# Cross-attention with layer norm: inverse roots as exp(-ln/2), and a new order for the last six row tiles

## The chip, the core and the metric

The kernel runs on one core of one Trainium2 chip. The metric is the device time of one execution in microseconds (us), lower is better. The engines have instruction queues of their own and meet through semaphores: TensorE (PE in the profile; PEld is its weight load), VectorE (DVE), ScalarE (ACT), GpSimd (POOL), and SyncE (SP), whose queue issues nearly all DMAs.

## The reference

Cross-attention of x (16 batches, 256 rows, 256 columns) to a context of 77 keys of 192 columns, 8 heads of 256, then a residual and a layer norm, all in float32:

```python
Q = (img_embed @ Wq).reshape(B, -1, H, D).transpose(0, 2, 1, 3)
K = (sent_embed @ Wk).reshape(B, -1, H, D).transpose(0, 2, 1, 3)
V = (sent_embed @ Wv).reshape(B, -1, H, D).transpose(0, 2, 1, 3)
score = jnp.einsum('bhqd,bhkd->bhqk', Q, K) / math.sqrt(D)
score = jnp.where(mask, score, -jnp.inf)
attn = jax.nn.softmax(score, axis=-1)
ctx = jnp.einsum('bhqk,bhkd->bqhd', attn, V).reshape(B, -1, H * D)
out = ctx @ Wo + img_embed
mu = jnp.mean(out, axis=-1, keepdims=True)
var = jnp.var(out, axis=-1, keepdims=True)
return (out - mu) * jax.lax.rsqrt(var + EPS) * gamma + beta
```

## The kernel before

**Tiling.** The 4,096 rows of x are 32 tiles of 128 rows, numbered 0 to 31, two to a batch and eight to a group; a group is one buffer `xg`, in which x, the residual sum and the output replace each other in place. The weights are folded first (Wq with Wk into `gA`, `gB`; Wv with Wo into `uA`, `uB`), which takes the first 55 us of the profile.

**The loop.** Lines 854 to 925 run over b from -1 to 14, software-pipelined by batch: `new` are the two tiles of batch b+1, which get scores, softmax and a transpose; `now` are the two of batch b, which get their attention product; `old` are the two of batch b-1, which get their layer norm. In the last iteration, b = 14, `old` is tiles 26 and 27, `now` 28 and 29, `new` 30 and 31. After the loop lines 929 to 945 attend tiles 30 and 31 and normalise 28 to 31. The order in which the program is written is the order on each engine's queue; nothing is rescheduled.

**The steps for one tile t**, with the engine that does each:

- `scores(t)`: 128 matmuls on PE into two PSUM banks.
- `shift(t)`: DVE adds the mask bias (L326, twice) and takes the negated maximum of each head (L333).
- `exponential(t)`: eight Exp on ACT, one for each head (L340).
- `weigh(t)`: DVE sums (L346) and inverts (L348), POOL multiplies (L354, twice).
- `turn(t)`: DVE transposes the weights for the product (L364).
- `attend(t)`: 40 matmuls on PE into one PSUM bank (L376). Batches 0 to 10 use `seven` in its place, a product with fewer multiplications.
- `finish(t)`: DVE adds the product to the residual (`add_product`, L474) where that has not been done, then takes mean and variance (bn_stats L482, bn_aggr L485) into `mv`.
- `spread(first, last)`: ACT takes std = Sqrt(var + eps) of tiles first to last-1 (L493).
- `invert(first, last, aside)`: DVE takes rstd = 1/std (L500); for the tiles in `aside`, `less` = -mean * rstd on POOL, or on the engine given as `less_on` (L504).
- `normalise(t)`: in one of two ways. On DVE alone: `centre` (L514, subtract the mean and multiply by gamma) and L530 (multiply by rstd, add beta), both scalar_tensor_tensor. Or `aside`: ACT applies rstd and `less` (Identity, L524), POOL multiplies by gamma (L525) and adds beta (L526). When both tiles of a batch are done, SP issues their output DMA (L537); the two last tiles have a DMA each (L945).

**ScalarE's tables.** Exp and Sqrt come from different sets of tables. Before an activation whose function is not in the loaded set stands an ACT_TABLE_LOAD; Copy and Identity follow either without one. The one-element Exp into `warm` (L598, L890, L911) brings Exp's set back at a time of the program's choosing.

**The end, in the order of the code.** Iteration 14 on DVE: `shift` 30 and 31, then statistics of 26 between the softmax sums of 30 and 31, those of 27, `turn(30)`, the reciprocal for 26 and 27, `turn(31)`, `finish` 28 and 29. On ACT: 16 Exp, Sqrt for 26 and 27, two copies of the product V*Wo of batch 15 out of PSUM (`vw`, L884), Identity of 26 and 27, Sqrt for 28 and 29. Behind the loop: 28 and 31 are normalised by DVE, 29 and 30 by ACT and POOL.

Of the kernel before, what the change touches and what calls it, by code (L numbers as in the profile page):

```python
# [8 lines left out]
F32 = mybir.dt.float32  # L9
I32 = mybir.dt.int32  # L10
AF = mybir.ActivationFunctionType
# [4 lines left out]
P = 128  # L16
# [37 lines left out]
def kernel(  # L54
# [13 lines left out]
    nc = tc.nc  # L68
    B, S, DI = x.shape
# [3 lines left out]
    NG = B // GB  # L73
    QT = S // P
    NT = B * QT
    GT = GB * QT
# [17 lines left out]
    const = ctx.enter_context(tc.tile_pool(name="const", bufs=1))  # L94
    sp = ctx.enter_context(tc.tile_pool(name="sp", bufs=2))
    st = ctx.enter_context(tc.tile_pool(name="st", bufs=4))
# [4 lines left out]
    eps = const.tile([P, 1], F32, tag="eps", name="eps")  # L101
# [22 lines left out]
    bias = const.tile([P, B, S2], F32, tag="bias", name="bias")  # L124
# [3 lines left out]
    xg_of = {}  # L128

    x_rows = x.rearrange("b (t p) d -> p (b t) d", p=P)  # L130
    out_rows = out.rearrange("b (t p) d -> p (b t) d", p=P)
    c_rows = c.rearrange("b k l -> (b k) l").rearrange("(r p) l -> p r l", p=CR)

    def flat(ap):
        return ap.rearrange("p a b -> p (a b)")
# [19 lines left out]
    xT_of, a_of, vw_of, p_of, mv_of = {}, {}, {}, {}, {}  # L155
# [142 lines left out]
    def turn_last(n):  # L298

        blocks = flat(vr[:, 2 * n : 2 * n + 2])  # L300
        nc.vector.transpose(blocks, blocks)


    def scores(t):
        g = t // GT
        j, bl = t % GT, (t // QT) % GB
        ps = [ps_mm.tile([P, 512], F32, tag="mm", name=f"ps_{t}_{a}") for a in range(2)]
        for m in range(NM):
            for dc in range(2):
                for i in range(NM):  # L310
                    nc.tensor.matmul(  # L311
                        ps[m // 2][i * BK : (i + 1) * BK, m % 2 * 2 * S2 : (m % 2 + 1) * 2 * S2],
                        xT_of[g][:, j * NM + m, dc],
                        flat(a_of[g][:, dc, bl, 2 * i : 2 * i + 2, :]),
                        start=(dc == 0),
                        stop=(dc == 1),
                    )
        ps_of[t] = ps
# [153 lines left out]
    def add_product(t):  # L472
        y = xg_of[t // GT][:, t % GT, :]
        nc.vector.tensor_tensor(y, po_of.pop(t), y, ALU.add)  # L474

    def finish(t):
        if t in po_of:
            add_product(t)
        g, j = t // GT, t % GT
        y = xg_of[g][:, j, :]  # L480
        bn = st.tile([P, 6], F32, tag="bn", name=f"bn_{t}")
        nc.vector.bn_stats(bn, y)  # L482
        if j == 0:
            mv_of[g] = st.tile([P, GT, 2], F32, tag="mv", name=f"mv_{g}", bufs=2)
        nc.vector.bn_aggr(mv_of[g][:, j, :], bn)  # L485

    std_of, rstd_of, done = {}, {}, []

    def spread(first, last):

        g, lo, hi = first // GT, first % GT, (last - 1) % GT + 1
        std = st.tile([P, GT], F32, tag="std", name=f"std_{first}")
        nc.scalar.activation(std[:, lo:hi], mv_of[g][:, lo:hi, 1], AF.Sqrt, bias=eps)  # L493
        std_of[first, last] = std

    def invert(first, last, aside=(), less_on=nc.gpsimd):

        g, lo, hi = first // GT, first % GT, (last - 1) % GT + 1
        rstd = st.tile([P, GT], F32, tag="rstd", name=f"rstd_{first}")
        nc.vector.reciprocal(rstd[:, lo:hi], std_of.pop((first, last))[:, lo:hi])  # L500
        if aside:
            less = st.tile([P, GT], F32, tag="less", name=f"less_{first}")
            for j in (t % GT for t in aside):
                less_on.tensor_scalar(  # L504
                    less[:, j : j + 1], mv_of[g][:, j, 0:1], rstd[:, j : j + 1], -1.0,
                    ALU.mult, ALU.mult,
                )
        for t in range(first, last):
            j = slice(t % GT, t % GT + 1)
            rstd_of[t] = rstd[:, j], less[:, j] if aside else None  # L510

    def centre(t):
        y = xg_of[t // GT][:, t % GT, :]
        nc.vector.scalar_tensor_tensor(  # L514
            y, y, mv_of[t // GT][:, t % GT, 0:1], gam, ALU.subtract, ALU.mult
        )

    def normalise(t, aside=False, centred=False):

        g, j = t // GT, t % GT  # L520
        rstd, less = rstd_of.pop(t)
        y = xg_of[g][:, j, :]
        if aside:
            nc.scalar.activation(y, y, AF.Identity, bias=less, scale=rstd)  # L524
            nc.gpsimd.tensor_tensor(y, y, gam, ALU.mult)  # L525
            nc.gpsimd.tensor_tensor(y, y, bet, ALU.add)  # L526
        else:
            if not centred:
                centre(t)
            nc.vector.scalar_tensor_tensor(y, y, rstd, bet, ALU.mult, ALU.add)  # L530
        if t >= NT - QT:
            return
        done.append(t)
        if t ^ 1 in done:
            t |= 1
            j |= 1
            nc.sync.dma_start(  # L537
                out_rows[:, t + 1 - QT : t + 1, :], xg_of[g][:, j + 1 - QT : j + 1, :]
            )
# [4 lines left out]
    with tc.tile_pool(name="wonce", bufs=1) as wp:  # L544
        first = -(-GB * S2 // CR)
# [48 lines left out]
            load_blocks(wk_blk[:, e], wk_blocks[2 * e + 1])  # L594
            load_blocks(wq_blk[:, e], wq_blocks[2 * e + 1])

        warm = const.tile([P, 1], F32, tag="warm", name="warm")
        nc.scalar.activation(warm, eps, AF.Exp)  # L598

        wvT = wp.tile([P, NF, NL, P], F32, tag="wvT", name="wvT")  # L600
        wo_of = [
# [251 lines left out]
    last = NT - 1  # L853
    for b in range(-1, B - 1):
        old = range(max(b - 1, 0) * QT, b * QT)
        now = range(max(b, 0) * QT, (b + 1) * QT)
        new = range((b + 1) * QT, (b + 2) * QT)
        for t in new:
            scores(t)
        for t in new:  # L860
            shift(t)
        for n in range(0, 2) if b < 0 else range(b + 2, min(b + 3, B // 2)):
            turn_last(n)
        g, n = (b + 1) // GB + 1, (b + 1) % GB
        work = [prepare_vw(b + 1)]
        if g < NG:
            work.append(prepare_a(g, (n,)))
            if n == 0:
                load_xT(g)
                load_x(g)  # L870
        for part_A, _, _ in work:
            part_A()
        for _, part_B, _ in work:
            part_B()
        for i, t in enumerate(new):
            exponential(t)
            if old:
                finish(old[i])
            weigh(t)
        if old:  # L880
            spread(old[0], old[-1] + 1)
        for _, _, copies in work:
            for dst, src in copies():
                nc.scalar.copy(dst, src)  # L884
        if b + 1 < NS:
            differences(b + 1)
        if b < NS:
            if now:
                seven(b)
            nc.scalar.activation(warm, eps, AF.Exp)  # L890
            if old:
                invert(old[0], old[-1] + 1)
                normalise(old[0])
            for t in new:
                turn(t)
            if n >= NF - 2:
                for j in range((n - NF + 2) * GT // 2, (n - NF + 3) * GT // 2, 2):
                    transpose_x(g, j)
            if old:
                normalise(old[1])  # L900
            if now:
                add_seven(b)
            if b + 1 < NS:
                sums(b + 1)
            continue
        for t in now:
            attend(t)
        if b < B - 2:
            invert(old[0], old[-1] + 1, aside=old[:1])
            normalise(old[0], aside=True)  # L910
            nc.scalar.activation(warm, eps, AF.Exp)  # L911
            turn(new[0])
            normalise(old[1])
            turn(new[1])
            for t in now:
                add_product(t)
        else:
            turn(new[0])
            invert(old[0], old[-1] + 1, aside=old)
            for t in old:  # L920
                normalise(t, aside=True)
            turn(new[1])
            for t in now:
                finish(t)
            spread(now[0], now[-1] + 1)

    for t in new:
        attend(t)  # L930
    centre(last - 3)
    invert(last - 3, last - 1, aside=(last - 2,), less_on=nc.vector)
    normalise(last - 2, aside=True)
    finish(last - 1)
    spread(last - 1, last)
    normalise(last - 3, centred=True)
    invert(last - 1, last, aside=(last - 1,), less_on=nc.vector)
    normalise(last - 1, aside=True)
    finish(last)
    spread(last, NT)  # L940
    centre(last)
    invert(last, NT)
    normalise(last, centred=True)
    for t, queue in ((last - 1, nc.scalar), (last, nc.sync)):
        queue.dma_start(out_rows[:, t, :], xg_of[NG - 1][:, t % GT, :])  # L945


# [29 lines left out]
```

## Time and profile before

| | |
|---|---|
| time, median of 4 runs | 277.99 us (277.84 to 278.28) |
| the profiled execution | 278.28 us, of which the span is 276.5 us |
| PE busy | 267.3 us, 97% of the span |
| DVE busy | 208.6 us, 75% |
| ACT busy | 165.4 us, 60% |
| POOL busy | 159.6 us, 58% |
| table loads on ACT | 28 of 1,283 ns: 14 for L493, 10 for L890, 3 for L911, 1 for L598 |

Time outside the span (1.78 us here) is what lies around the profiled instructions. A line of the timeline gives start and length in us, then engine, line, operation, output and inputs with their shapes; what stands in brackets at its end is how long the engine had been idle and who released it. Instructions of one engine that don't depend on each other overlap by some tens of nanoseconds, so a start can lie ahead of the end before it.

### The profile page before, as it was taken

Reading aid. Unit: us, or ns where it says so; the run is one execution under the profiler, and the core shown is the slowest. Engines: PE = TensorE matmul, PEld = TensorE weight load, DVE = VectorE, ACT = ScalarE, POOL = GpSimd, SP = SyncE. Lnnn points to the kernel's source line nnn. Section 1 sums busy time; section 2 is a strip of 40 time slices with the busy share of each in tenths; the row PEclk is TensorE's granted clock in tenths of the full one; section 3 lists DMA queues with packets and bytes.
Section 4 is the critical chain, followed back from the end, with each engine's and each line's share of the span. In section 5 each row is a group of like instructions: output and inputs, shape, how many; then the busy total and the mean of one; then the engine's idle time right before and its main releaser. Section 6 shows DMA issues by size and latency. Waiting matters only on the chain.

```text
span 276.5 us, 13238 instructions
## 1 busy us (share of the span) xinstructions
PE 267.3 (97%) x5908; PEld 190.6 (69%) x5908; DVE 208.6 (75%) x423; ACT 165.4 (60%) x443; POOL 159.6 (58%) x221
## 2 busy tenths in 40 slices
PE   6899999999999999999999999999999999999991
PEld 6756587876494949595958586868676767575660
DVE  0453866787748989878789887777788887788885
ACT  2303122255729585867676776768685857869762
POOL 1000004948677777787867878777777536235184
PEclk9999999999999999999999999999999999999998
DMA  6995988892000101930100009500001010110103
GB/s 178 238 206 166 323 125 175 240 200 103 4 6 2 43 2 46 226 119 4 43 2 16 29 5 196 187 6 30 17 2 40 5 40 6 39 41 2 40 4 114
DMA packets 40201, 22.61 MB, mean 82 GB/s; under 512 B 23168, under 2 KB 38608, under 8 KB 40144
## 3 DMA queue, kind: packets, MB, share of 16 engines
q1 hardware_dynamic: 40000, 21.64, 31.9%
q8 instruction: 46, 0.75, 1.1%
q10 hardware_dynamic: 144, 0.13, 0.1%
q14 instruction: 11, 0.09, 0.1%
HBM read 17.57 MB, written 4.19 MB: 79 GB/s over the span
## 4 chain that ended last, share of the span: by engine, by line
PE 87%; DVE 4%; DMA 3%; ACT 2%; POOL 1%; SPq 1%; issue 1%; POOLq 0%; ACTq 0%
PE ps L311 24%; PE pa L197 12%; PE pv L239 9%; PE po L427 9%; PE pm L427 7%; PE pa L211 6%; PE pv L250 6%; PE po L376 5%; DMA c_sb<-in_ctx_dram 3%; PE pu L701 3%; ACT e L340 2%; PE pw L715 1%; PE pgb L701 1%; PE pr L282 1%; PE pr L272 1%; POOL uB L827 1%
## 5 line engine op out<-in xcount | busy, mean ns | idle before, releaser
L340 ACT ACTIVATE e<-s,top 128x77 f32<-128x77 f32 x256 | 67.2, 347 | 51.8 <-DVE top L333 49.6
L354 POOL TENSOR_TENSOR p<-e,rden 128x512 f32<-128x512 f32 x64 | 45.8, 738 | 46.0 <-DVE rden L348 40.6
L311 PE MATMUL ps<-a,xT 128*32 128x154 f32 x2048 | 70.0, 294 | 0.0
L311 PEld LDWEIGHTS ps<-a,xT 128*32 128x32 f32 x2048 | 66.1, 110 | 1.7 <-issue 0.8
L326 DVE TENSOR_TENSOR s<-ps,bias 128x308 f32<-128x308 f32 x64 | 30.4, 474 | 16.9 <-PE ps L311 16.8
L197 PE MATMUL pa<-cA,gA 128*32 128x308 f32 x512 | 35.8, 423 | 0.0
L460 POOL TENSOR_TENSOR xg<-xg,m 128x256 f32<-128x256 f32 x33 | 24.2, 733 | 13.5 <-DVE xg L474 11.8
L197 PEld LDWEIGHTS pa<-cA,gA 128*32 128x32 f32 x512 | 16.4, 110 | 20.9 <-issue 7.9
L239 PE MATMUL pv<-uA,cA 128*32 128x512 f32 x256 | 30.4, 592 | 0.0
L364 DVE STREAM_TRANSPOSE pT<-p 128x640 f32<-128x640 f32 x32 | 25.6, 825 | 2.6 <-POOL p L354 2.6
L346 DVE TENSOR_REDUCE den<-e 128x8 f32<-128x616 f32 x32 | 24.7, 772 | 3.2 <-ACT e L340 3.2
L333 DVE TENSOR_REDUCE top<-s 128x8 f32<-128x616 f32 x32 | 25.4, 795 | 1.1
L390 POOL TENSOR_TENSOR ts<-vw 128x768 f32<-128x768 f32 x11 | 22.0, 1998 | 0.0
L211 PE MATMUL pa<-cB,gB 64*32 64x308 f32 x512 | 19.5, 420 | 0.0
L376 PE MATMUL po<-vw,pT 128*32 128x256 f32 x320 | 19.2, 380 | 0.0
L884 ACT COPY vw<-pv 128x512 f32<-128x512 f32 x32 | 16.9, 578 | 2.7 <-PE pv L250 2.7
L493 ACT ACT_TABLE_LOAD x14 | 18.0, 1283 | 0.3
L211 PEld LDWEIGHTS pa<-cB,gB 64*32 64x32 f32 x512 | 9.7, 107 | 11.3 <-issue 7.6
L250 PE MATMUL pv<-uB,cB 64*32 64x512 f32 x256 | 17.4, 601 | 0.0
L514 DVE SCALAR_TENSOR_TENSOR xg<-xg,mv,gam 128x256 f32<-128x256 f32 x25 | 17.2, 688 | 0.0
L884 ACT COPY a<-pa 128x308 f32<-128x308 f32 x48 | 16.6, 446 | 0.0
L376 PEld LDWEIGHTS po<-vw,pT 128*32 128x32 f32 x320 | 10.0, 110 | 9.5 <-DVE den L346 2.5
(118 smaller groups left out, 415.5 us busy)
## 6 DMA issues: line engine op xcount, KB each, us to landing
xT<-in_x_dram SPq DMA_DIRECT2D x16, 256.0 KB, 7.1
xg<-in_x_dram SPq DMA_DIRECT2D x4, 1024.0 KB, 7.7
out_dram<-xg SPq DMA_DIRECT2D x15, 256.0 KB, 2.1
wo<-in_L_xattn_Wo_dram SPq DMA_DIRECT2D x4, 512.0 KB, 6.3
wvT<-in_L_xattn_Wv_dram SPq DMA_DIRECT2D x16, 96.0 KB, 3.4
wq_nat<-in_L_xattn_Wq_dram SPq DMA_DIRECT2D x2, 512.0 KB, 6.4
wq_blk<-in_L_xattn_Wq_dram SPq DMA_DIRECT2D x8, 128.0 KB, 5.3
wk_blk<-in_L_xattn_Wk_dram SPq DMA_DIRECT2D x8, 96.0 KB, 5.8
```

Of the source, the lines that this page charges most:

```text
L197: nc.tensor.matmul(flat(o[i * BK : (i + 1) * BK]), gA[:, h, cols(dc, i)], flat(cA[:, batches, :]), start=not B_first, stop=B_first,)
L211: nc.tensor.matmul(flat(banks[j + k][i * BK : (i + 1) * BK]), gB[half(k), h % NF, cols(dc, i)], flat(cB[half(k), batches, :]), start=B_fir ...
L239: nc.tensor.matmul(pv[k][i * BK : (i + 1) * BK], cA[:, b, k * BK : (k + 1) * BK], uA[:, parts, :, i], start=True, stop=False,)
L250: nc.tensor.matmul(pv[k][i * BK : (i + 1) * BK], cB[half(k), b, k * BK : (k + 1) * BK], uB[half(k), parts, :, i], start=False, stop=True,)
L311: nc.tensor.matmul(ps[m // 2][i * BK : (i + 1) * BK, m % 2 * 2 * S2 : (m % 2 + 1) * 2 * S2], xT_of[g][:, j * NM + m, dc], flat(a_of[g][:, ...
L326: nc.vector.tensor_tensor(s[:, a * H // 2 : (a + 1) * H // 2], ps[a][:, : H // 2 * S2].rearrange("p (h k) -> p h k", k=S2), bias[:, b, :]. ...
L340: nc.scalar.activation(e[:, h], s[:, h], AF.Exp, bias=top[:, h : h + 1])
L354: nc.gpsimd.tensor_tensor(part, e_mh[:, :, :, keys], rden_mh.unsqueeze(3).to_broadcast(list(part.shape)), ALU.mult,)
L364: nc.vector.transpose(pT_of[t].rearrange("p n m q -> p m n q"), p.rearrange("p m (n k) -> p m n k", k=BK),)
L376: nc.tensor.matmul(po[i * BK : (i + 1) * BK], pT[:, n, i], vw_of[b][:, 2 - n // 2 * 2 : 4 - n // 2 * 2, n % 2, :] if n < NF else vr[:, b, ...
L427: nc.tensor.matmul(out[i * BK : (i + 1) * BK], weight[:, i], moving, start=(n == 0), stop=(n == len(terms) - 1),)
L884: nc.scalar.copy(dst, src)
```

## The change

- `spread` takes, in place of one Sqrt, a Ln of var + eps and an Exp of -0.5 times that, which is rstd itself. The reciprocal in `invert` goes; `invert` only makes `less`.
- The table set `natural_log_exp_and_others` is asked for once, at the start; the three warm Exp are gone.
- In iteration 14, `finish`, `spread`, `invert` and `normalise` of tiles 26 and 27 (both aside, `less` on POOL) stand between the scores and `shift` of tiles 30 and 31.
- The rest of iteration 14: `turn(30)`, `finish(28)`, `spread` of 28 alone, `turn(31)`.
- Behind the loop, 28 and 29 are normalised aside (ACT and POOL, `less` on DVE), one after the other, each with a spread of its own; 30 and 31 are each finished, spread, centred and normalised on DVE, and both output DMAs are issued by SP, each behind its tile.

```diff
     def spread(first, last):
         g, lo, hi = first // GT, first % GT, (last - 1) % GT + 1
-        std = st.tile([P, GT], F32, tag="std", name=f"std_{first}")
-        nc.scalar.activation(std[:, lo:hi], mv_of[g][:, lo:hi, 1], AF.Sqrt, bias=eps)
-        std_of[first, last] = std
+        log = st.tile([P, GT], F32, tag="log", name=f"log_{first}")
+        rstd = st.tile([P, GT], F32, tag="rstd", name=f"rstd_{first}")
+        nc.scalar.activation(log[:, lo:hi], mv_of[g][:, lo:hi, 1], AF.Ln, bias=eps)
+        nc.scalar.activation(rstd[:, lo:hi], log[:, lo:hi], AF.Exp, scale=-0.5)
+        all_rstd_of[first, last] = rstd
     def invert(first, last, aside=(), less_on=nc.gpsimd):
-        g, lo, hi = first // GT, first % GT, (last - 1) % GT + 1
-        rstd = st.tile([P, GT], F32, tag="rstd", name=f"rstd_{first}")
-        nc.vector.reciprocal(rstd[:, lo:hi], std_of.pop((first, last))[:, lo:hi])
+        g = first // GT
+        rstd = all_rstd_of.pop((first, last))
...
-        warm = const.tile([P, 1], F32, tag="warm", name="warm")
-        nc.scalar.activation(warm, eps, AF.Exp)
+        nc.scalar.preload_act_table_set("natural_log_exp_and_others")
...
         for t in new:
             scores(t)
+        if b == B - 2:
+            for t in old:
+                finish(t)
+            spread(old[0], old[-1] + 1)
+            invert(old[0], old[-1] + 1, aside=old)
+            for t in old:
+                normalise(t, aside=True)
         for t in new:
             shift(t)
...
         for i, t in enumerate(new):
             exponential(t)
-            if old:
+            if old and b < B - 2:
                 finish(old[i])
             weigh(t)
-        if old:
+        if old and b < B - 2:
             spread(old[0], old[-1] + 1)
...
-            nc.scalar.activation(warm, eps, AF.Exp)
...
-            nc.scalar.activation(warm, eps, AF.Exp)
...
         else:
             turn(new[0])
-            invert(old[0], old[-1] + 1, aside=old)
-            for t in old:
-                normalise(t, aside=True)
+            finish(now[0])
+            spread(now[0], now[1])
             turn(new[1])
-            for t in now:
-                finish(t)
-            spread(now[0], now[-1] + 1)
     for t in new:
         attend(t)
-    centre(last - 3)
-    invert(last - 3, last - 1, aside=(last - 2,), less_on=nc.vector)
-    normalise(last - 2, aside=True)
-    finish(last - 1)
-    spread(last - 1, last)
-    normalise(last - 3, centred=True)
-    invert(last - 1, last, aside=(last - 1,), less_on=nc.vector)
-    normalise(last - 1, aside=True)
-    finish(last)
-    spread(last, NT)
-    centre(last)
-    invert(last, NT)
-    normalise(last, centred=True)
-    for t, queue in ((last - 1, nc.scalar), (last, nc.sync)):
-        queue.dma_start(out_rows[:, t, :], xg_of[NG - 1][:, t % GT, :])
+    add_product(last - 2)
+    for t in (last - 3, last - 2):
+        invert(t, t + 1, aside=(t,), less_on=nc.vector)
+        normalise(t, aside=True)
+        if t < last - 2:
+            finish(t + 1)
+            spread(t + 1, t + 2)
+    for t in (last - 1, last):
+        finish(t)
+        spread(t, t + 1)
+        centre(t)
+        invert(t, t + 1)
+        normalise(t, centred=True)
+        nc.sync.dma_start(out_rows[:, t, :], xg_of[NG - 1][:, t % GT, :])
```

More of the change, by code (lines that the diff above doesn't have):

```diff
@@ L485, in finish @@
         nc.vector.bn_aggr(mv_of[g][:, j, :], bn)
-    std_of, rstd_of, done = {}, {}, []
+    all_rstd_of, rstd_of, done = {}, {}, []
     def spread(first, last):
         g, lo, hi = first // GT, first % GT, (last - 1) % GT + 1
-        std = st.tile([P, GT], F32, tag="std", name=f"std_{first}")
-        nc.scalar.activation(std[:, lo:hi], mv_of[g][:, lo:hi, 1], AF.Sqrt, bias=eps)
-        std_of[first, last] = std
+        log = st.tile([P, GT], F32, tag="log", name=f"log_{first}")
[3 more added lines that the diff above has]
+        all_rstd_of[first, last] = rstd
     def invert(first, last, aside=(), less_on=nc.gpsimd):
-        g, lo, hi = first // GT, first % GT, (last - 1) % GT + 1
-        rstd = st.tile([P, GT], F32, tag="rstd", name=f"rstd_{first}")
-        nc.vector.reciprocal(rstd[:, lo:hi], std_of.pop((first, last))[:, lo:hi])
+        g = first // GT
+        rstd = all_rstd_of.pop((first, last))
         if aside:
```

## The prediction

> **What bounds the kernel now.** First the busy times and the costliest groups:
>
> ```profile
> PE 267.3 (97%) x5908; PEld 190.6 (69%) x5908; DVE 208.6 (75%) x423; ACT 165.4 (60%) x443; POOL 159.6 (58%) x221
> L493 ACT ACT_TABLE_LOAD x14 | 18.0, 1283 | 0.3
> ```
>
> PE is the bound by far, and ACT, from which the change takes table loads, has 40% to spare. Whether the last stage differs is told by the chain of work that ended last (start, length, work):
>
> ```profile
> 247.82 1.72 PE pv L239 x16
> 249.54 1.02 PE pv L250 x16
> 250.56 4.45 PE po L376 x80
> 255.01 2.14 PE ps L311 x64
> ...
> 258.57 2.05 ACT e L340 x8
> ...
> 265.39 0.84 DVE pT L364
> 266.23 0.32 DVE xg L474
> ...
> 271.22 0.34 DVE xg L474
> ...
> 273.04 0.75 DVE xg L530
> ```
>
> From 49.4 to 257.15 this chain is matmuls without a gap. What other engines do up to there is hidden, as long as PE gets its operands. Then it passes through the softmax of 30 and 31 to `turn(31)` at 265.39, and from there to 273.79 it is DVE alone. So 8.4 us of the span are DVE's, and what leads to `turn(31)` decides their start. The timeline of the end gives the prices:
>
> ```profile
> 254.34 0.48 DVE L530 SCALAR_TENSOR_TENSOR xg<-xg,rstd,bet 128x256 f32<-128x256 f32 x1
> 262.79 1.28 ACT L493 ACT_TABLE_LOAD   x1
> 264.08 0.30 ACT L493 ACTIVATE std<-mv,eps 128x2 f32<-128x2 f32 x1
> 270.09 0.61 PE L376 MATMUL po<-vr,pT 128*32 128x256 f32 x8
> 271.93 0.72 POOL L525 TENSOR_TENSOR xg<-xg,gam 128x256 f32<-128x256 f32 x1 [0.45 <-ACT xg L524]
> 272.26 0.67 DVE L514 SCALAR_TENSOR_TENSOR xg<-xg,mv,gam 128x256 f32<-128x256 f32 x1
> 272.73 0.78 POOL L526 TENSOR_TENSOR xg<-xg,bet 128x256 f32<-128x256 f32 x1
> 273.04 0.75 DVE L530 SCALAR_TENSOR_TENSOR xg<-xg,rstd,bet 128x256 f32<-128x256 f32 x1
> 273.82 0.35 SPq L945 DMA_DIRECT2D out_dram<-xg  x1
> ```
>
> PE ends at 270.70, so nothing after the change can add tile 31's product before about 270.76. DVE's L514 and L530 take 0.44 and 0.48 alone (minima 0.442 and 0.484 of 25), but 0.67 and 0.75 here. Both end 0.28 after the POOL instruction that they overlap (272.65 and 273.51), and so do L514 at 268.12 and L530 at 270.09: the DVE instruction gets going when POOL's has ended. From L530's end to the span's end it is 2.71.
>
> **The change, part by part.** *Table loads.* 28 loads become one: 27 x 1.283 = 34.6 us of ACT time, and 15 warm Exp of 0.20. Cover: the PE chain up to 257.15. The loads of the last stage (255.09 and 262.79) stand in idle time of ACT or behind the last exponential, with the `vw` copies done at 265.34 and wanted at 266.20. Price on the path: 0. Were ACT the bound, it would be the 34.6.
>
> The Trainium skill (*ScalarE: Activation LUTs*, section "What ACT_TABLE_LOAD costs") charges a drain of 1,380 ns for each switch besides the 1,283. The Sqrt above starts 0.01 behind its load, so the row shows no drain; by the page the switches would be worth 72 us of ACT in place of 34.6, and on the path 0 by either.
>
> *Ln and Exp for Sqrt and reciprocal.* Neither is in the trace. Ln has the operands of the Sqrt, 0.295; bounds 0.20 (one-column Exp of L890) and 0.60 (Identity on 256 columns). The Exp has the form of L890's, 0.20; upper bound 0.35 (L340). It reads what Ln wrote, and dependent neighbours elsewhere start 0.03 after the end. From the start of bn_aggr: 0.21 to Ln, 0.295, 0.03, 0.20, 0.05 to the consumer: 0.79. DVE no longer waits 0.57 for std (L500, 13 times); in the loop that is hidden by PE.
>
> *Tiles 26 and 27 ahead of the exponentials.* Iteration 13 first: `turn(28)` need not wait for rstd, so it starts at 252.37 in place of 253.12. `centre(25)` and L530 then meet POOL's products of 29, which costs about 0.35 of that. I take 0.35 as left (bounds 0 and 0.4): `finish(26)` starts at F = 256.15 - 0.35 = 255.8, where `shift(30)` stood. Two finishes are 2 x 0.56 = 1.12 of DVE, and `shift(30)` is queued behind them; its second half waits for PE to 257.17 anyway, so the maxima of 30 end near 258.7 (before: 258.49). On ACT, 16 exponentials are now queued behind the normalise: bn_aggr of 27 starts at F+1.02, Ln +0.21, Exp +0.32, `less` on POOL +0.28, Identity +0.30 (265.33 to 265.63), and +1.0 for two of them: F+3.13 = 258.93. Call s the delay of the first exponential: 258.93 - 258.57 = 0.36, taken as 0.4. The maxima alone would give 0.15, F at 256.15 gives 0.7. POOL's four instructions for 26 and 27 run from 258.6 to 261.7, in its idle 5.49 before the product of 30. Their DMA goes out near 261.7 in place of 269.45, on an idle SP: 0. DVE loses the statistics that stood ahead of the sums of 30, so these start at 261.04 either way.
>
> *Up to tile 31's product.* `turn(31)` comes at 265.39+s by POOL's product, or by DVE's own queue (`turn(30)`, add, bn_stats, bn_aggr of 28: 263.75 + s + 0.72 + 0.42 + 0.46 + 0.10) at T = 265.45+s. PE wants its output at 268.36: slack 2.9 less its 0.84, so PE doesn't wait. The `vw` copies move ahead, as 1.58 of load and Sqrt go. From T: turn 0.77, add of 29 0.33, `less` of 28 at L = T+1.10. POOL then multiplies and adds for 28 from L+0.93 and for 29 from L+2.43 (0.25 to Identity, 0.68 to POOL, pitch 0.81 and 0.69). DVE: `less` of 29 waits for its Exp until L+1.37, add of 30 L+1.50 (or 268.6, when PE has it), statistics, `centre(30)` at L+2.61. That is behind POOL's product of 29, which lasts to L+3.16: `centre` ends at L+3.43. L530 of 30 starts at L+3.46, behind POOL's add of 29, which ends near L+4.01: done at L+4.29. The add of 31 follows at A = L+4.21 = 270.75+s = 271.15. Before: 271.13. So one pair of DVE instructions still meets POOL, and two reciprocals, a `less` and the statistics ahead of the sums are paid for by s.
>
> The Trainium skill speaks against this order: *SBUF — State Buffer*, section "Who interferes with whom", has a VectorE instruction with two SBUF inputs fully blocked for the whole of a GpSimd instruction that started first. The four endings above agree; in the worst phase by the page each of the two would lose all of POOL's 0.73, or 1.46 together, where I have 0.38+0.35.
>
> *The tail.* Before, from the add of 31: 0.45+0.46 to bn_aggr, 1.00 to L530, 0.75: 2.66. After, POOL is done at L+4.01 = 270.96, so `centre(31)` and L530 run alone: 0.45+0.46, 0.79 to 0.86 to rstd (Sqrt came 0.28 behind the last bn_aggr), 0.485: 2.2. L530 ends at 271.15+2.2 = 273.35 in place of 273.79: -0.44.
>
> *Output.* SP issues 28/29 near 271.0 and 30 near 271.4 (0.37 each), so both are clear of 31's issue. Before, the 128 KB of 30 and 31, issued 0.27 apart, shared the DMA engines from 274.4 to 275.2. Alone, the last should land about 0.1 earlier (bounds 0 and 0.3). -0.10.
>
> Sum: -0.44 - 0.10 = -0.54, or s - 0.94 in general: break-even at s = 0.94. The profiled execution would take 278.28 - 0.54 = 277.74; it lies 0.29 above the median, so the forecast for the median is **277.45**.
>
> **The rivals.** *A, more is gained.* `centre(30)` comes 0.2 earlier and goes ahead of POOL's product of 29; then its L530 ends at L+3.85, and A falls to PE's bound of 270.76: -0.93, 277.06. For it: the two are 0.18 apart in my sum. Against: the add of 30 can't start before 268.6.
>
> *B, the gain is eaten.* F stays at 256.15 and the normalise of 26 and 27 holds ACT a little longer: s = 0.9, 277.95. For it: the 0.35 of iteration 13 is my softest number.
>
> *C, slower.* The place is ACT's queue ahead of the first exponential of 30. Costs: F late (0.40), `less` at 0.48, as four of the five on POOL took about that, with the second Identity behind it (0.21), Ln and Exp at their high bounds, some 0.7 with pitch. From 0.31 that makes s = 1.62, +0.68: 278.67. It decides from s = 0.94 and shows as slower from s = 1.5. Against: all three have to come together.
>
> *D, it doesn't do what it says.* If Ln and Exp were still served from two sets, each of the five last spreads would pay 2 x 1.283. One stands ahead of the exponentials (s = 3.0), one behind the last bn_aggr: 3.0 - 0.94 + 2.57 = +4.6, 282.6 at least. For it: nothing in the trace shows such a set. Against: Copy and Identity already follow either Exp or Sqrt without a load.
>
> **How the numbers follow.** Forecast 0.52, its own range 277.1 to 277.8; A 0.18, B 0.14, C 0.13, D 0.03. A measurement of this kernel tells about 0.2%, 0.56 us, from no change. The forecast lies on that edge: 0.30 of its 0.52 below 277.43, 0.22 above. Faster: 0.30+0.18 = 0.48; same: 0.22+0.14 = 0.36; slower: 0.16. The range reaches from A with a shorter Ln (276.95) to between B and C (278.35).
>
> **What would show it.** One ACT_TABLE_LOAD in all; the first exponential of 30 near 258.97; `turn(31)` near 265.85 with PE unbroken to 270.70; L514 and L530 of 31 at 0.44 and 0.48, of 30 at 0.7 or more; L530 of 31 ending near 273.35. I am wrong if PE pauses ahead of 270.70, if POOL still works on 29 after 272, or if s is over 0.94.

## The result, and the profile after

The changed kernel is slightly slower: 278.9 us (median), against 278.2 us for the kernel before on the same chips. The ratio is 1.0025, with a 95% interval of 1.0014 to 1.0035. The profiled execution took 278.63 us with a span of 276.8 us (before: 278.28 and 276.5), so the span shows +0.3, about half of the +0.7 in the medians. The forecast was a ratio of 277.45/277.99 = 0.9981: the wrong direction, and 278.9 lies outside the range.

The page of the changed kernel begins as the change says. ACT is busy for 131.9 us in place of 165.4, and the group of table loads that stood at L493 is gone. The third line is new to the story: "q1" is the DMA queue that carries all data, and its last column is the time that its packets took, as a share of 16 engines' span. "q8" is taken here for the queue that brings PE its instructions, in blocks: 46 packets of 16 KB, about 257 of PE's 5,908 matmuls and 5,908 weight loads to each.

```profile
PE 267.9 (97%) x5908; PEld 191.4 (69%) x5908; DVE 210.2 (76%) x406; ACT 131.9 (48%) x419; POOL 160.3 (58%) x221
...
q1 hardware_dynamic: 40144, 21.77, 35.7%
q8 instruction: 46, 0.75, 1.2%
```

The same line of the page before:

```profile
q1 hardware_dynamic: 40000, 21.64, 31.9%
```

Nearly the same bytes took 35.7% in place of 31.9%. The change adds no transfer: the 144 packets are those of tile 30's output, which ScalarE's queue issued before and SP issues now. Something made the packets themselves slower.

**The end got shorter, as forecast.** The timeline of the changed kernel, for the instructions that the prediction put times to:

```profile
259.94 4.10 ACT L340 ACTIVATE e<-s,top 128x77 f32<-128x77 f32 x16
...
266.71 0.81 DVE L364 STREAM_TRANSPOSE pT<-p 128x640 f32<-128x640 f32 x1
...
270.25 0.73 POOL L526 TENSOR_TENSOR xg<-xg,gam 128x256 f32<-128x256 f32 x1
270.79 0.48 DVE L515 SCALAR_TENSOR_TENSOR xg<-xg,mv,gam 128x256 f32<-128x256 f32 x1
271.06 0.80 POOL L527 TENSOR_TENSOR xg<-xg,bet 128x256 f32<-128x256 f32 x1
271.37 0.77 DVE L531 SCALAR_TENSOR_TENSOR xg<-xg,rstd,bet 128x256 f32<-128x256 f32 x1
...
273.19 0.48 DVE L515 SCALAR_TENSOR_TENSOR xg<-xg,mv,gam 128x256 f32<-128x256 f32 x1
273.19 0.29 ACT L494 ACTIVATE log<-mv,eps 128x1 f32<-128x1 f32 x1 [1.87 <-DVE mv L485]
273.51 0.20 ACT L495 ACTIVATE rstd<-log 128x1 f32<-128x1 f32 x1
273.77 0.48 DVE L531 SCALAR_TENSOR_TENSOR xg<-xg,rstd,bet 128x256 f32<-128x256 f32 x1
```

DVE's L515 and L531 of tile 31 take 0.48 each (0.67 and 0.75 before), side by side with Ln and Exp on ACT. From the end of PE's last matmul to the end of the span it is 276.8 - 271.73 = 5.07, where it was 276.5 - 270.70 = 5.80: **0.73 less**.

**But PE comes to the end 1.03 later** (271.73 against 270.70). The chain of waits says where. The changed kernel, in the iteration that starts its `seven` product (L427) near 118 us:

```profile
118.06 1.88 PE pm L427 x64
119.94 1.40 PE po L427 x49
121.34 0.53 issue
121.87 0.97 PE po L427 x28
```

The kernel before, same place:

```profile
118.11 1.88 PE pm L427 x64
119.99 2.18 PE po L427 x80
122.18 4.19 PE ps L311 x128
```

Before, the 80 matmuls follow each other in 2.18. After, PE stops in the middle of a group, behind the 49th of 80, waiting for nothing that the profile shows: no semaphore wait is seen. PE restarts slowly too (28 matmuls in 0.97, 35 ns each, against 27 ns before), and what follows in this iteration comes 1.09 later against the start of `pm` than before. PE had begun its first scores 0.05 earlier, and nothing later makes the rest good: +1.03 - 0.73 = +0.3, the difference of the spans.

At that time the DMA engines are busy with the loads of group 2 of x: four strided loads into `xT` (the transposed x, in 256-byte packets) and one of 1 MB into `xg`. The DMA view from 108 to 121 us shows, in 40 slices, the engines' busy share in tenths, and the share of q1 in the stretch. First before, then after:

```profile
DMA  0000199899999999999999899989999994101000
...
q1 hardware_dynamic: 5472, 2.36, 80.4%
```

```profile
DMA  0004999999999999999999999999999999951100
...
q1 hardware_dynamic: 5472, 2.36, 96.6%
```

The same 5,472 packets and 2.36 MB start a slice earlier, keep the engines full without a dip, and end two slices (0.65 us) later. So two facts call for a reason: slower packets, and a pause of PE that no semaphore explains.

**A candidate.** `warm`, a tile of 4 bytes in each partition, is gone, and with it a slot of 32 bytes in front of the buffers allocated behind it. The compiled programs place `xg` at byte 73,472 of each partition before and at 73,440 after, and `xT` at 133,504 and 133,472; the weights move likewise. 73,472 and 133,504 are multiples of 64; the new addresses are 32 off. Theory A is then: packets that land 32 bytes off a multiple of 64 take longer, the burst ends later, a PE instruction block waits behind it, PE runs out of instructions. The other theories are B, the new tables (something in Ln and Exp, or in DVE being done earlier, disturbs PE), C, the new order at the end, and D, chance of the execution. These letters have nothing to do with those of the prediction's rivals.

### The profile page after: what moved, and what is told of

The parts are those of the page before. It is cut to its first block, busy times and chain, and to the rows that moved or that the text cites. A ratio compares the mean times of both kernels' runs of the same rounds, so it can differ in the third digit from the quotient of the medians.

```text
span 276.8 us, 13206 instructions
## 1 busy us (share of the span) xinstructions
PE 267.9 (97%) x5908; PEld 191.4 (69%) x5908; DVE 210.2 (76%) x406; ACT 131.9 (48%) x419; POOL 160.3 (58%) x221
## 3 DMA queue, kind: packets, MB, share of 16 engines
q1 hardware_dynamic: 40144, 21.77, 35.7%
## 4 chain that ended last, share of the span: by engine, by line
PE 93%; DMA 3%; DVE 2%; SPq 1%; issue 0%; DVEq 0%
PE ps L311 24%; PE pa L197 12%; PE pv L239 10%; PE po L427 9%; PE pm L427 7%; PE po L376 7%; PE pa L211 6%; PE pv L250 6%; DMA c_sb<-in_ctx_dram 3%; PE pu L701 3%; PE pr L272 2%; PE pgb L701 1%; PE pw L715 1%; PE pr L282 1%; PE phb L715 1%; PE ph L758 1%
## 5 line engine op out<-in xcount | busy, mean ns | idle before, releaser
L354 POOL TENSOR_TENSOR p<-e,rden 128x512 f32<-128x512 f32 x64 | 47.2, 758 | 43.8 <-DVE rden L348 29.8
L197 PEld LDWEIGHTS pa<-cA,gA 128*32 128x32 f32 x512 | 17.1, 110 | 20.2 <-issue 7.3
L531 DVE SCALAR_TENSOR_TENSOR xg<-xg,rstd,bet 128x256 f32<-128x256 f32 x25 | 19.2, 768 | 2.3 <-ACT vw L891 0.5
L390 POOL TENSOR_TENSOR ts<-vw 128x768 f32<-128x768 f32 x11 | 20.2, 1840 | 0.0
L474 DVE TENSOR_TENSOR xg<-po,xg 128x256 f32<-128x256 f32 x32 | 12.1, 414 | 7.1 <-PE po L427 6.5
```

The source lines that it names most:

```text
L197: nc.tensor.matmul(flat(o[i * BK : (i + 1) * BK]), gA[:, h, cols(dc, i)], flat(cA[:, batches, :]), start=not B_first, stop=B_first,)
L354: nc.gpsimd.tensor_tensor(part, e_mh[:, :, :, keys], rden_mh.unsqueeze(3).to_broadcast(list(part.shape)), ALU.mult,)
```

## The experiments

Ratios are to the kernel before on the same chip, with 95% intervals. "Pause" is what the iterations between 108 and 136 us lost on PE, "end" is from PE's last matmul to the end of the span, both from the profile of that run.

| run | ratio | span | q1 | pause | end |
|---|---|---|---|---|---|
| s1_before_again | 0.9996 [0.9979, 1.0013] | 276.3 | 33.1% | 0.52 | 5.76 |
| s1_after_again | 1.0015 [0.9991, 1.0039] | 278.0 | 35.1% | 0.97 | 5.11 |
| s1_tables_only | 1.0017 [0.9997, 1.0036] | 277.0 | 34.6% | 1.48 | 5.44 |
| s1_order_only | 0.9968 [0.9942, 0.9995] | 276.4 | 30.1% | 0 | 5.38 |
| s2_before_shift32 | 1.0063 [1.0042, 1.0084] | 278.0 | 34.5% | 1.73 | 5.81 |
| s2_after_pad32 | 0.9952 [0.9932, 0.9973] | 274.8 | 31.5% | 0 | 5.11 |
| s2_tables_pad32 | 0.9963 [0.9943, 0.9983] | 276.4 | 32.3% | 0.30 | 5.41 |
| s2_after_pad512 | 0.9948 [0.9931, 0.9966] | 274.7 | 29.6% | 0 | 5.13 |
| s3_xT_off | 1.0013 [0.9987, 1.0039] | 277.4 | 33.5% | 1.01 | 5.08 |
| s3_xg_off | 0.9973 [0.9945, 1.0001] | 275.0 | 33.3% | 0.06 | 5.14 |
| s3_split | 0.9964 [0.9938, 0.9990] | 276.1 | 34.4% | 0 | 5.23 |
| s3_best | 0.9940 [0.9916, 0.9963] | 274.8 | 30.1% | 0 | 5.15 |
| s4_before_split | 0.9977 [0.9954, 1.0000] | 275.6 | 32.3% | 0 | 5.90 |
| s4_tables_split | 0.9947 [0.9927, 0.9967] | 275.6 | 31.9% | 0 | 5.43 |
| s4_after_split | 0.9955 [0.9936, 0.9973] | 276.4 | 31.7% | 0 | 5.21 |

Spans of single executions scatter by up to about 1 us from things that have nothing to do with the question: the first scores matmul comes between 54.3 and 55.8 us, as the load of the context lands early or late. That is why pauses and ends are read beside them.

"Pause" leaves out what PE lost elsewhere. Between its first scores matmul and its first `pm`, near 60 us, PE lost another 1.49 in `s1_after_again`, 1.31 in `s3_xT_off`, 0.76 in `s3_split`, 0.35 in `s2_before_shift32` (which lost a further 0.24 near 184 us) and 0.12 in `s4_after_split`; the other profiles lost nothing there. All but the last of these have `xT` 32 off.

**The two halves of the change, and both kernels once more.** `s1_tables_only` takes the new tables in the old order; `s1_order_only` keeps Sqrt, reciprocal and `warm` up to tile 25 and has Ln/Exp and the new order behind.

```diff
 # s1_tables_only, against the kernel before
-        nc.scalar.activation(std[:, lo:hi], mv_of[g][:, lo:hi, 1], AF.Sqrt, bias=eps)
+        nc.scalar.activation(log[:, lo:hi], mv_of[g][:, lo:hi, 1], AF.Ln, bias=eps)
+        nc.scalar.activation(rstd[:, lo:hi], log[:, lo:hi], AF.Exp, scale=-0.5)
...
-        warm = const.tile([P, 1], F32, tag="warm", name="warm")
-        nc.scalar.activation(warm, eps, AF.Exp)
+        nc.scalar.preload_act_table_set("natural_log_exp_and_others")
```

```diff
 # s1_order_only, against the kernel before; the new order as in the change
+        if first < NT - 6:
             std = st.tile([P, GT], F32, tag="std", name=f"std_{first}")
             nc.scalar.activation(std[:, lo:hi], mv_of[g][:, lo:hi, 1], AF.Sqrt, bias=eps)
             std_of[first, last] = std
+            return
...
-            nc.scalar.activation(warm, eps, AF.Exp)
+            if b < B - 3:
+                nc.scalar.activation(warm, eps, AF.Exp)
+            else:
+                nc.scalar.preload_act_table_set("natural_log_exp_and_others")
```

> Tiles 0 to 25 keep Sqrt, reciprocal and the warm Exp; from tile 26 on Ln and Exp and the new order. Theory 1 (the loss is made in the middle, where the kernel without Sqrt lets PE wait for its instructions, and the new end gains): PE unbroken up to 257, the end as in the changed kernel (5.07 us from PE's last matmul to the span's end in place of 5.80), so about 0.5 us faster than before, ratio near 0.998. Theory 2 (the pause of PE at 121 to 127 us in the profile is chance, and the new end is what loses): ratio near 1.0025, as the changed kernel.

> Ln and Exp and one table load throughout, the order of the kernel before. Theory 1: the middle of the changed kernel without the new end, so about 1 to 1.4 us slower than before, ratio near 1.004 to 1.005, with a pause of PE somewhere between 50 and 180 us. Theory 2: ratio between 0.998 and 1.000.

> The changed kernel once more. Theory 1: ratio near 1.0025, and PE pauses again while x of a later group is loaded (50 to 60, 109 to 120 or 165 to 180 us). Theory 2: ratio near 1.0025, and no pause in this profile.

> The kernel before under a new label: ratio 1.000 within what a measurement tells; it shows how far a profile of the same kernel moves. Theory 1: no pause of PE, or a shorter one than in the changed kernel. Theory 2: pauses like those of the changed kernel.

The end shortens by 5.80 - 5.44 = 0.36 from the tables alone and by 5.80 - 5.38 = 0.42 from the order, together 0.78, about the 0.73 of both. The pause goes with the tables, not with the order, as theory 1 has it; but the 1.0017 of `s1_tables_only` lies between the forecasts of the two theories. The repeats of both kernels speak against D: 0 and 0.52 in the two profiles of before, 1.09 and 0.97 in those of after. But this does not part A from B. `s1_tables_only` has no `warm`, so it lies 32 bytes off; and `s1_order_only`, which has new tiles in a pool ahead of `xT`, happens to lie at 133,632, a multiple of 512. Its low q1, 30.1%, speaks for addresses; it doesn't settle them.

**32 bytes alone, from both sides.** A tile of 32 bytes that nothing reads or writes puts `warm`'s place back into the changed kernel; the same tile behind `warm` pushes the kernel before 32 off.

```diff
 # s2_after_pad32, against the changed kernel; s2_tables_pad32 likewise, against s1_tables_only
         nc.scalar.preload_act_table_set("natural_log_exp_and_others")
+        const.tile([P, 8], F32, tag="pad", name="pad")
```

```diff
 # s2_before_shift32, against the kernel before
         warm = const.tile([P, 1], F32, tag="warm", name="warm")
+        const.tile([P, 8], F32, tag="pad", name="pad")
```

```diff
 # s2_after_pad512: s2_after_pad32, and 128 bytes more ahead of xT, which then lies at a multiple of 512
     all_rstd_of, rstd_of, done = {}, {}, []
+    st.tile([P, 32], F32, tag="pad_st", name="pad_st", bufs=1)
```

> The changed kernel with 32 unused bytes where the buffer warm was, so that every buffer behind it lies where it lay before. Theory A (the 32 bytes are the loss: DMAs to buffers that start 32 bytes off a multiple of 64 take longer, and PE's instructions wait behind them): packets back to 32% of the DMA engines' span from 35.7%, no pause of PE over 0.6 us at 121 us, ratio 0.997 to 0.998. Theory B (the loss comes from the new arithmetic, which lets VectorE finish and SyncE issue the loads of x earlier): 35 to 36%, ratio 1.0015 to 1.0025 as without the pad.

> Ln and Exp and one table load in the old order, with the same 32 bytes. Theory A: 32% and a ratio of 0.999 to 1.000, since the table loads were hidden. Theory B: ratio 1.0015 or more, as without the pad (1.0017).

> The kernel before with 32 unused bytes more behind warm, nothing else. Theory A: 35 to 36% of the DMA engines' span, a pause of PE near 121 us, 1 to 1.4 us slower, ratio 1.003 to 1.005. Theory B: ratio 1.000 and 32%.

> The changed kernel with the 32 bytes and 128 more ahead of the transposed x, which then starts on a multiple of 512 bytes, as in the kernel with the new order alone (0.9968). Theory A, with more gained at 512: 30% or less, ratio 0.995 to 0.997. Theory A, with 64 bytes enough: as the first kernel of this set. Theory B: 1.0015 to 1.0025.

The chain of waits of `s2_before_shift32`, with the instructions of the kernel before, has the pause behind the same 49th matmul:

```profile
119.51 1.40 PE po L427 x49
120.91 1.43 issue
122.35 0.97 PE po L427 x28
```

and that of `s2_after_pad32`, with the instructions of the changed kernel, has none:

```profile
117.11 1.89 PE pm L427 x64
118.99 2.18 PE po L427 x80
121.17 4.19 PE ps L311 x128
```

The share of q1 goes with the address as well. `s2_before_shift32`:

```profile
q1 hardware_dynamic: 40000, 21.64, 34.5%
```

and `s2_after_pad32`:

```profile
q1 hardware_dynamic: 40144, 21.77, 31.5%
```

32 unused bytes make the kernel before 0.63% slower, and turn the changed kernel from 1.0025 [1.0014, 1.0035] to 0.9952 [0.9932, 0.9973], faster than before. B falls as the cause of the pause: Ln and Exp are in `s2_after_pad32` too. The direction is that of theory A in every run, but three of its sizes were too small: 1.0063 where 1.003 to 1.005 was expected, 0.9952 where it was 0.997 to 0.998, and 0.9963 for `s2_tables_pad32` where it was 0.999 to 1.000. A boundary of 512 bytes lowers q1 further, to 29.6%, but its ratio of 0.9948 can't be told from 0.9952.

**Which buffer, and by which way.** `s3_xT_off` has `xT`, the weights and what lies behind them 32 off and `xg` in place; `s3_xg_off` the reverse. `s3_split` leaves everything 32 off, as in the changed kernel, but loads the 1 MB of a group's `xg` in four parts of 256 KB, one in each iteration, so that the burst is 0.75 MB smaller. `s3_best` has the split and the addresses of `s2_after_pad512`.

```diff
 # s3_xT_off, against the changed kernel; s3_xg_off has the first tile alone
+    st.tile([P, 8], F32, tag="pad_st", name="pad_st", bufs=1)
...
         nc.scalar.preload_act_table_set("natural_log_exp_and_others")
+        const.tile([P, 8], F32, tag="pad", name="pad")
```

```diff
 # s3_split, against the changed kernel
-    def load_x(g):
-        xg_of[g] = const.tile([P, GT, DI], F32, tag=f"xg{g}", name=f"xg_{g}")
-        nc.sync.dma_start(xg_of[g], x_rows[:, g * GT : (g + 1) * GT, :])
+    def load_x(g, n=None):
+        if not n:
+            xg_of[g] = const.tile([P, GT, DI], F32, tag=f"xg{g}", name=f"xg_{g}")
+        js = slice(0, GT) if n is None else slice(n * QT, (n + 1) * QT)
+        nc.sync.dma_start(xg_of[g][:, js], x_rows[:, g * GT + js.start : g * GT + js.stop, :])
...
                 load_xT(g)
-                load_x(g)
+            load_x(g, n)
```

> The changed kernel with xg where it lay before (a multiple of 64 bytes), and the transposed x, the weights and c 32 bytes off. If the many small packets of the transposed x (256 bytes each) carry the loss: their mean near 30 ns, those of 1,024 bytes near 52 ns, a pause of PE near 121 us, ratio 1.000 to 1.002. If xg carries it: no pause, ratio 0.995 to 0.997.

> The opposite: xg 32 bytes off, the transposed x, the weights and c where they lay before. If the transposed x carries the loss: 256-byte packets near 22 ns, those of 1,024 bytes near 60 ns, no pause, ratio 0.995 to 0.997. If xg carries it: pause near 121 us, ratio 1.000 to 1.002.

> The changed kernel with every buffer 32 bytes off as in the change, but each group's 1 MB of xg loaded in four parts of 256 KB, one to an iteration, in place of all at once behind the transposed x. If PE waits because its instruction blocks queue behind that burst: packets still 35% of the DMA engines' span, but no pause near 121 us, ratio 0.995 to 0.997. If slow packets cost PE in another way: ratio 1.001 to 1.003 still.

> The changed kernel with the pads of 32 and 128 bytes and the split loads: no pause in any profile, packets near 30%, ratio 0.994 to 0.996, not measurably better than with the pads alone (0.9948), since that profile had no pause left.

`xT` off gives the loss (1.0013, pause 1.01), `xg` off alone hardly any (0.9973, pause 0.06). The intervals of the two ratios just touch. The chain of `s3_xT_off` has the pause, behind the 49th matmul again, as in all seven profiles whose pause is 0.3 or more:

```profile
118.73 1.88 PE pm L427 x64
120.62 1.40 PE po L427 x49
122.02 0.71 issue
122.73 0.97 PE po L427 x28
```

That of `s3_xg_off` has none:

```profile
117.21 1.88 PE pm L427 x64
119.10 2.25 PE po L427 x80
```

The four loads of `xT` between 108 and 121 us take longer to land (the last number, a median in us). First `s3_xT_off`, then `s3_xg_off`:

```profile
xT<-in_x_dram SPq DMA_DIRECT2D x4, 256.0 KB, 7.2
```

```profile
xT<-in_x_dram SPq DMA_DIRECT2D x4, 256.0 KB, 5.9
```

The packets themselves don't tell the two apart. Their mean was expected near 30 and 52 ns (256 and 1,024 bytes) with `xT` off, and near 22 and 60 with `xg` off; it was 25 and 51, and 24 and 53, with q1 at 33.5% and 33.3%. So that `xT` carries the loss is read from pauses, ratios and landings, and why is not shown: `xT` arrives in 16,384 packets of 256 bytes, `xg` in 4,096 of 1,024, and a charge for each packet would fall on `xT` most. The weights moved with `xT`, and weren't moved alone.

`s3_split` parts the busy queue from the pause. The share of q1 stays high:

```profile
q1 hardware_dynamic: 40288, 21.77, 34.4%
```

but its chain of waits has no gap near 121 us (its lines are two further down than those of the changed kernel):

```profile
118.29 1.89 PE pm L429 x64
120.17 2.18 PE po L429 x80
122.35 4.19 PE ps L313 x128
```

All that moved lies 32 off in this run too, its ratio is 0.9964, and `pm` and `po` take the same 1.89 and 2.18 as elsewhere, so the loss is not that the engines read or write slower at such addresses. A high share of q1 alone costs nothing in this iteration; it costs where it holds up what PE needs. What that is, the packets of q8 suggest. Some three blocks are fetched in an iteration, and in every run the 17th block of the execution comes near the start of this `pm`. The moment it has landed, counted from there, goes with the pause:

```
block starts + lasts (us from pm's start) -> pause of PE
s3_split          -0.23 + 1.11 -> 0
s1_order_only     +0.32 + 0.94 -> 0
before            +0.36 + 0.94 -> 0
s2_after_pad512   +0.55 + 0.93 -> 0
s2_after_pad32    +0.57 + 0.96 -> 0
s3_xg_off         +0.68 + 1.07 -> 0.06
s2_tables_pad32   +0.88 + 0.93 -> 0.30
s1_before_again   +1.15 + 1.05 -> 0.52
s1_after_again    +1.37 + 1.11 -> 0.97
after             +1.41 + 1.14 -> 1.09
s3_xT_off         +1.64 + 0.94 -> 1.01
s1_tables_only    +2.10 + 1.14 -> 1.48
s2_before_shift32 +2.27 + 1.14 -> 1.73
```

A block that is in by some 1.7 us costs nothing or next to it; each tenth later is about a tenth of pause. In `s3_best` and the three runs of the next set it is in by 1.0, and none pauses there. The kernel before lies close to that edge (1.30 in one execution, 2.20 in the other), and 32 bytes push it over.

The losses near 60 us, one of which `s3_split` has, follow the same order. In `s3_split` it is 4.55 from the start of the first line to that of the last:

```profile
59.21 1.96 PE pv L241 x14
61.16 0.35 PE pa L199 x4
61.51 0.17 PE pv L241
61.68 2.08 PE pa L199 x21
63.76 1.02 PE pv L252 x16
```

and in the kernel before 3.79:

```profile
59.79 1.72 PE pv L239 x16
61.51 2.07 PE pa L197 x32
63.58 1.02 PE pv L250 x16
```

Counted from the first scores matmul, the block that comes there has landed by 2.66 in the twelve profiles that lose nothing, and at 2.82, 2.99, 3.50, 4.20 and 4.23 in those that lose 0.12, 0.35, 0.76, 1.49 and 1.31. So late blocks and pauses go together at two places; no run delayed a block by itself, and why a block starts late (it lasts 0.9 to 1.5 everywhere) is not shown.

**Is the shorter end all of the gain?** `s2_after_pad32` gains 0.0048 x 278.2 = 1.3 us, but its end is only some 0.7 shorter. If the kernel before loses some 0.6 to its own pauses, the split must give it that, and leave between the three kernels their ends alone.

```diff
 # s4_before_split: the kernel before with the edit of s3_split
 # s4_tables_split: s2_tables_pad32 with it
 # s4_after_split:  s2_after_pad32 with it
-                load_x(g)
+            load_x(g, n)
```

> The kernel before with xg of each group loaded in four parts. If the kernel before pauses now and then for its instructions: 0.4 to 0.8 us faster, ratio 0.997 to 0.9985, no pause in the profile. If it doesn't: ratio 1.000.

> Ln and Exp in the old order, addresses as before, split load. If pauses are the missing 0.6 us: 0.4 us (0.0014) below the kernel before with the split load, ratio 0.9955 to 0.997. If the new arithmetic gains in another way: 0.9935 or less, or 1.0 us below it.

> The changed kernel, addresses as before, split load. If pauses are the missing part: 0.7 us (0.0025) below the kernel before with the split load, ratio 0.994 to 0.996; if not, 1.3 us below it.

`s4_before_split` is 0.0023 x 278.2 = 0.64 faster than before, just the size wanted, though its interval reaches 1.0000. Behind the split the tables should lie 0.0014 below it and got 0.9977 - 0.9947 = 0.0030; the whole change should lie 0.0025 below it and got 0.0022. With intervals of 0.002 on either side the first is neither confirmed nor refuted. So it fits that the remaining 0.6 of `s2_after_pad32` are the pauses of the kernel before, but it **stays open**.

Eight versions have their whole interval below the kernel before. The lowest are the changed one with `xT` at a multiple of 512 and the split (0.9940), the tables with pad and split (0.9947), the changed one with `xT` at a multiple of 512 (0.9948) and with 32 bytes in `warm`'s place alone (0.9952). Their intervals overlap; the last is one line.

## Why the prediction was wrong, point by point

**The step that failed** is the first: "28 loads become one: 27 x 1.283 = 34.6 us of ACT time, and 15 warm Exp of 0.20 … Price on the path: 0". The instructions were priced (the Exp that went are 16: 12 of L890, 3 of L911, 1 of L598), the buffer that went with them was not. Removing `warm` moved every later buffer by 32 bytes, and that is worth +0.63% on the kernel before (`s2_before_shift32`) and 1.0025 - 0.9952 = 0.73% on the changed one (two comparisons, of ratios with intervals of 0.1 to 0.2% to either side). Of 278.2 us that is 2.0, nearly four times the gain forecast; the 1.03 of the profile is what one execution lost at one place. The rivals missed it with the forecast: all four stand in the last stage or on ACT's queue, while the loss stands at 121 us, on PE. "From 49.4 to 257.15 this chain is matmuls without a gap" was true of that execution (another of the same kernel, `s1_before_again`, paused for 0.52), and it was taken as cover that couldn't fail, as long as PE had its operands. By the order of blocks and pauses above, PE needs its instructions in time too. "I am wrong if PE pauses ahead of 270.70" named the sign, though not its cause.

**The same step, second part:** "DVE no longer waits 0.57 for std (L500, 13 times); in the loop that is hidden by PE". PE is not the only one behind DVE. SP's queue holds the output DMA, which waits for DVE, ahead of the loads of x. Those loads are issued 9.3 ahead of the start of `pm` in the changed kernel and 9.0 before. No run isolates what these 0.3 are worth; the right address made the loss vanish with them in place.

**The end was right in mechanism, and larger than the sum.** Times of the changed kernel less 1.03, the lateness of PE:

- First exponential of 30: 258.91, forecast 258.97; s = 0.34, taken as 0.4.
- `turn(31)`: 265.68, forecast 265.85.
- Ln 0.28 to 0.30 and Exp 0.20, 0.03 apart: as priced. One table load in all, so the prediction's rival D fell.
- `centre(30)` was forecast behind POOL's product of 29. It took 0.48 and ended 0.29 after that product, so it met POOL, but lost only some 0.04. L531 of 30 took 0.77 and ended 0.28 after POOL's add of 29: as forecast. The Trainium skill (*SBUF — State Buffer*, section "Who interferes with whom") has such a DVE instruction blocked until GpSimd's has ended; both endings agree with it. The worst case worked out from it, 1.46, did not come: 0.04 + 0.29.
- L515 and L531 of 31 alone: 0.48 and 0.48, forecast 0.44 and 0.48.
- L531 of 31 ended at 273.22, forecast 273.35: the term of -0.44 measured -0.57.
- Output, L531's end to the span's end: 2.55 in place of 2.71, so -0.16 where -0.10 was taken.

Together -0.73 in place of -0.54. The prediction's rivals B and C, a first exponential late by 0.9 or 1.62, didn't come about either: the slower side was right only as an outcome.

## What to carry to other kernels

A tile that is removed or added moves every buffer behind it: compare the addresses before and after, and the share of time that the same bytes take on the data queue, before a loss is looked for in the instructions that changed. An engine that pauses in the middle of a group of its own, with no semaphore to wait for, may be out of instructions; look for the instruction queue's packets beside a burst of loads. Where a burst of small packets runs under a saturated engine, try its destination on a multiple of 64, and the burst spread over iterations; here each was worth 0.5% or more to the changed kernel.

## What the runs showed of the hardware that was not expected

**The address of the destination.** Mean time of a packet in the burst between 104 and 124 us, for 256 and 1,024 bytes: 24 and 53 ns before, 30 and 59 in `s2_before_shift32`; 30 and 58 in the changed kernel, 20 and 53 in `s2_after_pad32`. In `s2_after_pad512`, on a multiple of 512, it is 20 and 51. The address alone doesn't set these means: the kernel before had 27 and 55 in `s1_before_again`, with nothing moved, and with `xT` 32 off the 256-byte packets took 25 in `s3_xT_off` and 26 in `s3_split`. What 32 bytes cost the whole kernel is shown from both sides; a price for one packet is not. The Trainium skill (*DMA: Bandwidth & Descriptors*, section "How a descriptor splits into AXI transactions") has a charge for reads that don't start on a multiple of 256 bytes. What moved here is where the loads write, and no such step at 256 shows in this burst: `xT` of `s2_after_pad32` lies 128 off a multiple of 256 and takes 20 ns, as on a multiple of 512, though q1's share of the whole run is 31.5 against 29.6%.

**PE can run dry.** The Trainium skill (*Runtime: NRT & Kernel Launch*, section "Instruction fetch mechanics") has the engines stream instructions in blocks of 16 KiB, 256 instructions, over a DMA queue of their own, with the crossing from block to block mostly hidden. The block size agrees with q8's 46 packets in 0.75 MB. Mostly hidden it is not here, if q8 is read rightly: blocks come late while the loads of x keep the DMA engines busy, and PE lost up to 1.73 us in one iteration.
